# The expert layers of a mixture-of-experts block, computed on the transposed side, with the gate weights fetched by copy and the token weights found from the tokens' side

## The chip, the cores and the metric

One core of one Trainium2 chip runs the whole kernel. The number that counts is the device time of one execution in microseconds (us). The span in a profile is the time from the first to the last instruction of a core.

The engines are called PE (matrix products and transposes; PEld is its loading of weights), ACT (activations and copies), DVE (elementwise work and reductions), POOL (here nearly only indirect DMAs, and some elementwise steps) and SP (it issues the direct DMAs). Each has a queue of its own and takes its instructions in order.

## The reference, cut to what matters

The input is 16 batches of 512 tokens of 128 numbers. Each batch passes an attention layer with 16 heads and then a mixture of 160 experts, of which each token uses 8.

```python
h = layernorm(x) * (1 + ca) + sa;   x = x + ga * attention(h)
h = layernorm(x) * (1 + cb) + sb;   x = x + gb * ffn(h)

def ffn(x):                                     # x: tokens x 128
    probs = sigmoid(x @ router_w.T + expert_bias)      # tokens x 160
    top_w, top_idx = top_k(probs, 8)
    top_w = 2.5 * top_w / (sum(top_w) + 1e-9)
    # for each of a token's 8 experts e with weight w:
    #   routed += w * (silu(x @ w_gate[e].T) @ w_down[e].T)     64 inner numbers
    shared = silu(x @ w_gate_shared.T) @ w_down_shared.T
    return routed + shared
```

## The kernel before

**Two stages.** From 0 to about 974 us the kernel computes attention for the 16 batches, 64 groups of four heads in all. In the gaps of that work it also routes finished batches. From 974 us on it runs the loop over the *quads*, which is the expert layer, and ends with a tail in which only gathers are left.

**Routing.** `route` (lines 520 to 593) computes the router's logits of a batch, turns them into `key = -(1 + exp(-logit))`, finds the 8 largest per token, makes a mask `m` of them and, from their reciprocals, one factor per token (`scale`). The batches form groups of 4, 4, 4, 3 and 1. When all batches of a group are routed, `place` (595 to 718) sorts the group's (token, expert) pairs into *slots*. Two neighbouring experts make a *pair*; a block of 128 slots belongs to one pair, so that one product of 128 columns serves both experts of it. `place` writes, per slot, which of the two halves has to be masked (`away`, from `lim`), and which pair each block has (`pid`).

**Scatter and gather.** Each routed batch is copied to its slots in DRAM by 32 indirect DMAs (`scattering`, line 741: 4 blocks of 128 tokens by 8 experts). After a group's quads, 32 indirect DMAs per batch fetch the results back (`gathering`, line 950), eight to a tile `got`. `combine` (962) adds these eight, multiplies by the token's factor and the gate, and adds the sum to the residual `xr`. There are 512 scatters and 512 gathers. All are issued by POOL.

**A quad** is four blocks of 128 slots. There are 190 in the main loop (44, 44, 44, 36 and 22 in the five groups) and a few spare ones behind a branch. One quad goes through these stages, each in another turn of the loop:

- `load` fetches 512 slots (`xs`), `load_down` the down weights of four pairs (`wd`); both are direct DMAs of 256 KB on SP's queue.
- `turn`: four PE transposes; ACT copies them to `xT`.
- `up`: for each of the four blocks a product with `xT` as the stationary operand and the pair's gate weights, straight out of the resident table `wg` at an address from a register, as the moving one (130 columns: two more hold the router's columns of the pair). After each comes a bf16 product with `away` that adds a huge negative number to the half that does not belong to the slot. DVE adds `shift` to the two router columns (`z`), and ACT applies Silu to the rest (`su`).
- `begin_weights` and `end_weights`: six small DVE steps and one of ACT per two quads find each slot's own weight `w` from `z`.
- `back`: four PE transposes of `su`; DVE copies them to `hwT`.
- `down`: four products with `hwT`; DVE multiplies the result by `w` into `y`, and SP stores it.

**The order** of the work is written out by the loop at line 1160, one turn per quad, with the stages of different quads side by side. Before the `down` of a quad PE reads eight numbers into registers (`name_up`, `name_down`). Side work (routing, placing, the shared expert) is kept in a list of generators, of which `steps.tick` runs up to two steps a turn.

**The planner** (`Steps`, line 1217) keeps a planned time: products advance it (`steps.work`), and it may never lie more than `AHEAD` = 3 us behind the planned ends of DVE and ACT. The `Pacer` (994) emits indirect DMAs by that planned time:

```python
def __call__(self):
    while steps.now >= self.due:
        self.due = max(self.due, steps.now - 4 * self.pace) + self.pace
        if stream(*self.sources) is None:
            break
```

In the quad loop the pace is `PACE_SLOTS` = 0.9 planned us per indirect DMA, scatters first and gathers when no scatter is ready. Each of these DMAs waits for the last PE instruction that was emitted before it (`paced`, 227). `add_up(LAG)` (1151) emits a `combine` as soon as more than `LAG` = 4 complete sets of eight gathers are emitted, so that DVE meets it some sets later; at the end of the loop it takes the rest.

```python
for i in range(-3, len(quads) + 7):
    for stage, q in (("load", i + 3), ("load_down", i - 3), ("name_up", i - 1),
                     ("name_down", i - 5), ("end_weights", i - 4), ("begin_weights", i - 3),
                     ("turn", i), ("up", i - 2), ("back", i - 4), ("down", i - 6)):
        ...
    prepare_sums(); steps.tick(); pacer(); add_up(LAG)
```

Helpers that record nearly all work share their lines: products stand on line 104, transposes on 111, DVE's and ACT's steps on 1212.

Of the kernel before, what the change touches and what calls it, by code (L numbers as in the profile page):

```python
# [19 lines left out]
NB = 16  # L20
S = 512
# [17 lines left out]
TINY = 1e-30  # L39
LAG = 4  # L40

PACE, PACE_SLOTS = 1.3, 0.9
# [28 lines left out]
def block_kernel(ctx: ExitStack, tc: tile.TileContext, t: dict, out: bass.AP):  # L71
# [88 lines left out]
    def load_rest():  # L160
        c.wrout = load("wroutT", [D, E])
        c.wgs = load("wgsT", [D, I])
        c.wds = load("wdsT", [I, D])
        c.bias_p = load("bias_p", [NC, 2])
        c.ones = load("ones", [P, 1])
        c.earlier = load("earlier", [P, P], BF)
        c.many = load("many", [1, P], BF)
        c.pairs = load("pairs", [NC, 2, NC])
        c.spread = load("spread", [NC, 2, E])
        c.table = load("table", [P, 2, NKM])  # L170
# [316 lines left out]
    rows = [tc.dram_tile([P, NBLK, D], FP, name=f"rows{b}") for b in range(NB)]  # L487

    somes = const.tile([1, len(GROUPS)], I32, tag="somes", name="somes")

    class Group:
        def __init__(self, g):
# [4 lines left out]
            self.scale = sb.tile([P, self.tb], FP, tag=f"scale{g}", name="scale")  # L497
            self.idx = sb.tile([P, self.tb, TOPK], I32, tag=f"idx{g}", name="idx")
            self.shift = sb.tile([P, self.nk, 2], FP, tag=f"shift{g}", name="shift")
            self.pid = sb.tile([1, self.nq, 9], I32, tag=f"pid{g}", name="pid")  # L500
            self.some = somes[:, g : g + 1]
            self.away = sb.tile(
                [P, -(-2 * self.nk // P), P], BF, tag=f"away{g}", name="away"
            )
            self.m, self.before = [], []
            self.xg = tc.dram_tile([self.nk * P, D], FP, name=f"xg{g}")
# [13 lines left out]
    def route(gr, i):  # L520
# [40 lines left out]
        yield  # L561

        top = sb.tile([P, NBLK, TOPK], FP, tag="top", name="top")
        for j in range(NBLK):
            vec.max(top[:, j, :], key[:, j, :])
            vec.match_replace(
                out=key[:, j, :], in_to_replace=top[:, j, :], in_values=key[:, j, :], imm_value=1.0
            )
            if j % 2:
                yield  # L570
        m = sb.tile([P, NBLK, E], BF, tag="m", name="m", bufs=max(GROUPS) + 2)
        vec.tensor_scalar(m, key, 0.0, None, ALU.is_gt)
# [13 lines left out]
        yield  # L586

        rs = gr.scale[:, i * NBLK : (i + 1) * NBLK]
        vec.reciprocal(top, top)
        vec.tensor_reduce(rs, top, AX.X, ALU.add, negate=True)  # L590
        vec.tensor_scalar(rs, rs, TOPK_EPS, None, ALU.add)
        vec.reciprocal(rs, rs)
        vec.tensor_scalar(rs, rs, ROUTED, None, ALU.mult)

    def place(gr):
# [41 lines left out]

# [58 lines left out]
        lim = gr.shift[:, :nk, :]  # L696
# [6 lines left out]
        vec.tensor_scalar(lim, lim, 1.0, FAR, ALU.subtract, ALU.mult)  # L703

        flat = tmp([P, 2 * NKM], BF, "flat")[:, : 2 * nk]
        vec.tensor_copy(flat, lim.rearrange("p n a -> p (n a)"))
        yield "o"
        pa = bank([P, -(-2 * NKM // P) * P], BF)
        for n, c0 in enumerate(range(0, 2 * nk, P)):
            k = min(P, 2 * nk - c0)  # L710
            turned(pa[:k, n * P : (n + 1) * P], flat[:, c0 : c0 + k], c.identb)
            vec.tensor_copy(gr.away[:k, n, :], pa[:k, n * P : (n + 1) * P])
        yield "o"
        for a in range(2):
            pl = bank([P, nk])
            mm(pl, c.bias_p[:, a : a + 1].broadcast_to([NC, P]), of)
            vec.tensor_tensor(lim[:, :, a], pl, lim[:, :, a], ALU.add)
            yield "o"
# [40 lines left out]
    class Quad:  # L759
# [17 lines left out]
        ALONE = {"xs": "a", "xT": "b", "su": "a", "wd": "c", "hwT": "b", "y": "a"}  # L777
# [11 lines left out]

        def load_down(self):  # L790
            (p0,) = self.numbers(SP, 0, 1, NC - 4)
            self.wd = self.tile([P, 4, D], "wd", 5)
            nc.sync.dma_start(out=self.wd, in_=t["wdT"][:, bass.ds(p0, 4), :])

        def turn(self):
            pt = now.ps.tile([P, S], FP, tag="turn", name="turn")
# [5 lines left out]
        def name_up(self):  # L802
            self.pids = self.numbers(PE, 1, 4, NC - 1)

        def up(self):

            pu = bank2().rearrange("p a (j n) -> p (a j) n", j=2)
            for j in range(4):
                mm(
                    pu[:, j, 0 : P + 2],  # L810
                    self.xT[:, j * P : (j + 1) * P],
                    wg[:, bass.ds(self.pids[j], 1), :].rearrange("p o n -> p (o n)"),
                    j % 2 == 0,
                    False,
                )
                n, k = divmod(4 * self.q + j, P // 2)
                rows_ = min(P, 2 * self.gr.nk - n * P)
                mm(
                    pu[:, j, 0:P].rearrange("p (a i) -> p a i", a=2),
                    self.gr.away[:rows_, n, :],  # L820
                    c.identb[:rows_, 2 * k : 2 * k + 2].unsqueeze(2).broadcast_to([rows_, 2, I]),
                    False,
                    j % 2 == 1,
                )

            if self.alone or self.q % 2 == 0:
                self.z = self.tile([P, 2, 4, 2], "z", 3)
            else:
                self.z = self.other.z
            vec.tensor_tensor(  # L830
                self.z[:, self.q % 2],
                pu[:, :, P : P + 2],
                self.gr.shift[:, 4 * self.q : 4 * self.q + 4, :],
                ALU.add,
            )
            self.u = self.tile([P, 4, P], "su", 3)
            act.activation(self.u, pu[:, :, 0:P], AF.Silu)

        def begin_weights(self):

            if self.q % 2 == 0 and not self.alone:
                return
            of = slice(self.q % 2, self.q % 2 + 1) if self.alone else slice(0, 2)
            z = self.tile([P, 2, 4], "z1", 3)
            self.w = self.tile([P, 2, 4], "w", 4)
            if not self.alone:
                self.other.w = self.w
            self.s = self.tile([P, 2, 4], "sz", 3)
            z, w = z[:, of], self.w[:, of]
            vec.tensor_tensor(z, self.z[:, of, :, 0], self.z[:, of, :, 1], ALU.max)  # L850
            vec.tensor_scalar(w, z, 0.0, TINY, ALU.is_equal, ALU.mult)
            vec.tensor_tensor(z, z, w, ALU.add)
            vec.reciprocal(w, z)
            act.activation(self.s[:, of], z, AF.Silu)

        def end_weights(self):
            if self.q % 2 or self.alone:
                of = slice(self.q % 2, self.q % 2 + 1) if self.alone else slice(0, 2)
                vec.tensor_tensor(self.w[:, of], self.w[:, of], self.s[:, of], ALU.mult)

        def back(self):
            pt = now.ps.tile([P, S], FP, tag="back", name="back")
            for j in range(4):
                turned(pt[:, j * P : (j + 1) * P], self.u[:, j, :], c.ident)
            self.hT = self.tile([P, S], "hwT", 3)
            vec.tensor_copy(self.hT, pt)
# [4 lines left out]
        def down(self):  # L871
            py = now.ps.tile([P, S], FP, tag="down", name="down")
            for j in range(4):
                mm(
                    py[:, j * D : (j + 1) * D],
                    self.hT[:, j * P : (j + 1) * P],
# [3 lines left out]
            vec.tensor_tensor(  # L880
                y,
                py.rearrange("p (n d) -> p n d", d=D),
                self.w[:, self.q % 2].unsqueeze(2).broadcast_to([P, 4, D]),
                ALU.mult,
            )
# [4 lines left out]
    def spare_quads(gr):  # L890
# [5 lines left out]
        with tc.If(some != 0):  # L896
            for q in range(gr.nq - spare(gr.size), gr.nq):
                quad = Quad(gr, q)
                quad.alone = True
                for stage in ("load", "load_down", "turn", "name_up", "up", "name_down"):  # L900
                    getattr(quad, stage)()
                quad.begin_weights()
                quad.end_weights()
# [508 lines left out]
```

## Time and profile before

| | us |
|---|---|
| median of 3 runs | 1918.97 (1918.86 to 1922.9) |
| the profiled execution | 1925.86 |
| its span | 1924.1 |
| PE busy | 1584.2 |
| DVE busy | 1253.8 |
| ACT busy | 826.6 |
| POOL busy | 1117.9 |

The profiled execution is 6.9 us above the median, and its span is 1.8 us below its own time. Mean granted clock of PE over the span: 0.934. POOL's busy time holds only the executing part of an indirect DMA; a further 0.30 us passes between two of them even when nothing is waited for.

### The profile page before, as it was taken

What the parts mean: (1) busy time and instruction counts of PE and PEld (TensorE: products, weight loads), DVE (VectorE), ACT (ScalarE), POOL (GpSimd) and SP (SyncE); (2) the same over time, 40 slices, a digit from 0 to 9 for tenths busy, and PEclk for the clock granted to TensorE, in tenths of its full rate; (3) what the DMA queues carried; (4) which work ended last, traced back from release to release, by engine and by line L of the source; (5) the groups of instructions that cost most, each with busy time, mean ns of one, the idle gap of its engine ahead of it and who ended that gap; (6) DMA issues with size and microseconds to landing.
All of it is one profiled execution on the core that took longest, in us unless ns stands there. A gap on an engine that the chain in (4) does not pass through costs nothing. (4 is left out here: it accounts for less than half of the span.)

```text
span 1924.1 us, 38397 instructions
## 1 busy us (share of the span) xinstructions
PE 1584.2 (82%) x12683; PEld 1133.7 (59%) x12747; DVE 1253.8 (65%) x3325; ACT 826.6 (43%) x1366; POOL 1117.9 (58%) x1139
## 2 busy tenths in 40 slices
PE   2799999998999989999888887888898878878700
PEld 1355555554555545555468776777788777777600
DVE  2677888887788867787636554546576656666622
ACT  1366666655666556664544332333233323323100
POOL 4001111047775477845657476777777777777776
PEclk8799999998999999999999898999899989999855
DMA  2456555565676667843257676778688878878622
GB/s 83 105 175 201 170 174 170 163 197 177 191 234 188 199 192 219 262 127 117 77 185 244 197 251 203 240 246 275 214 266 272 258 225 272 255 251 254 196 58 57
DMA packets 246678, 377.03 MB, mean 196 GB/s; under 512 B 37604, under 2 KB 136261, under 8 KB 246469
## 3 DMA queue, kind: packets, MB, share of 16 engines
q1 hardware_dynamic: 213700, 307.17, 51.4%
q0 software_dynamic: 32768, 67.17, 12.1%
q8 instruction: 119, 1.95, 0.4%
q14 instruction: 91, 0.74, 0.1%
HBM read 195.15 MB, written 178.26 MB: 194 GB/s over the span
## 5 line engine op out<-in xcount | busy, mean ns | idle before, releaser
L741 POOL DMA_INDIRECT xg<-hs,idx x512 | 493.4, 964 | 284.5 <-issue 95.0
L950 POOL DMA_INDIRECT got<-yg,idx x512 | 491.5, 960 | 156.7 <-issue 123.5
L1212 DVE TENSOR_REDUCE mins<-s 128x2 f32<-128x1024 f32 (+3 forms) x448 | 395.9, 913 | 123.5 <-PE s L104 121.7
L1212 ACT ACTIVATE pT<-s 128x1024 f32<-128x1024 f32 x320 | 323.0, 1021 | 176.7 <-PE s L104 172.3
L104 PE MATMUL s<-wg,xT 128*128 x1520 | 279.6, 307 | 0.6 <-issue 0.6
L104 PEld LDWEIGHTS s<-wg,xT 128*128 128x128 f32 x1520 | 241.6, 200 | 11.3 <-issue 1.2
L111 PE MATMUL turn<-ident,xs 128*128 128x128 f32 x760 | 123.8, 287 | 121.8 <-issue 49.7
L104 PE MATMUL s<-krep,qrep 96*128 96x512 bf16 (+3 forms) x1024 | 197.8, 306 | 31.9 <-DMA qrep<-parts 19.0
L104 PE MATMUL down<-wd,hwT 128*128 x1520 | 206.6, 280 | 3.7 <-DVE y L1212 3.7
L235 POOL TENSOR_TENSOR rot<-rot,three 128x512 f32<-128x512 f32 x32 | 36.8, 1160 | 291.4 <-ACT three L1212 289.4
L104 PE MATMUL s<-qrep,krep 128*128 128x128 bf16 (+3 forms) x960 | 181.6, 299 | 25.3 <-DVE mins L1212 12.3
L104 PE MATMUL av<-pT,v 128*32 128x512 f32 (+3 forms) x2048 | 193.4, 449 | 0.0
L104 PEld LDWEIGHTS down<-wd,hwT 128*128 128x128 f32 x1520 | 190.8, 197 | 4.1 <-DVE y L1212 4.0
L1212 ACT COPY xT<-turn 128x512 f32<-128x512 f32 x190 | 109.8, 578 | 164.8 <-PE turn L111 161.8
L111 PEld LDWEIGHTS turn<-ident,xs 128*128 128x128 f32 x760 | 85.6, 145 | 156.8 <-issue 116.4
L1212 DVE TENSOR_TENSOR z<-s,shift 128x8 f32<-128x8 f32 x190 | 29.6, 156 | 219.3 <-PE s L104 206.5
L104 PEld LDWEIGHTS <-identb 128*128 128x128 bf16 x1280 | 122.0, 100 | 84.9 <-issue 7.0
L104 PE MATMUL s<-identb,away 128*128 128x128 bf16 (+1 forms) x760 | 171.2, 225 | 0.0
L1212 ACT ACTIVATE su<-s 128x512 f32<-128x512 f32 x190 | 113.6, 598 | 129.3 <-DVE z L1212 121.8
L1212 DVE COPY hwT<-back 128x512 f32<-128x512 f32 x190 | 131.0, 689 | 44.2 <-PE back L111 43.6
L1212 DVE TENSOR_TENSOR y<-down,w 128x512 f32<-128x512 f32 x190 | 131.2, 691 | 38.5 <-PE down L104 33.6
L104 PEld LDWEIGHTS <-qrep 96*128 96x128 bf16 x1024 | 83.6, 99 | 119.7 <-issue 95.5
(179 smaller groups left out, 2356.6 us busy)
## 6 DMA issues: line engine op xcount, KB each, us to landing
xg<-zeros SPq DMA_DIRECT2D x228, 256.0 KB
xs<-xg SPq DMA_DIRECT2D x190, 256.0 KB
wd<-in_wdT SPq DMA_DIRECT2D x190, 256.0 KB
yg<-y SPq DMA_DIRECT2D x190, 256.0 KB
krep<-parts SPq DMA_DIRECT2D x64, 288.0 KB
qrep<-parts SPq DMA_DIRECT2D x192, 96.0 KB
parts<-three SPq DMA_DIRECT2D x96, 128.0 KB
yg<-zeros SPq DMA_DIRECT2D x38, 256.0 KB
```

What stands on the lines that cost most here:

```text
L104: steps.last = nc.tensor.matmul(out_, lhsT=lhsT, rhs=rhs, start=start, stop=stop).ins
L111: steps.last = nc.tensor.transpose(out_, in_, ident).ins
L235: in_order(getattr(nc.gpsimd, op)(*args).ins)
L741: s = nc.gpsimd.indirect_dma_start(out=gr.xg, out_offset=bass.IndirectOffsetOnAxis(ap=gr.idx[:, NBLK * i + j, k : k + 1], axis=0), in_=h[: ...
L950: s = nc.gpsimd.indirect_dma_start(out=got[:, k, :], out_offset=None, in_=gr.yg, in_offset=bass.IndirectOffsetOnAxis(ap=gr.idx[:, NBLK * i ...
L1212: return getattr(self.engine, op)(*args, **kwargs)
```

## The change

The first layer is computed transposed. `fetch_up` copies the four pairs' gate weights of a quad into a tile `wq`, two with ACT and two with DVE, each at an address from a register of that engine; PE no longer reads these numbers. In `up` the copied weights are the stationary operand and `xT` the moving one, so that the result has the 128 inner numbers as partitions and can be the stationary operand of `down` as it is: `back` and `hwT` are gone. The mask comes from one bf16 product of two rows (`half`, 2 x 128, with `hide`, 2 x 512) per quad. `hide` is written to DRAM by `place` and fetched for two quads at a time by `load_hide`. `down` no longer weighs; ACT copies its result.

The weights move to the tokens' side: `route` stores `key` and the mask in DRAM, and a new generator `weights` per batch takes them back, finds the eight weights of a token in the order of its eight gathers and normalizes them. `combine` multiplies the eight gathered rows by them before it adds. The pace goes from 0.9 to 0.75, `LAG` from 4 to 3, and some buffer counts change.

```diff
-LAG = 4
-PACE, PACE_SLOTS = 1.3, 0.9
+LAG = 3
+PACE, PACE_SLOTS = 1.3, 0.75
# route
+        nc.sync.dma_start(out=keys[b], in_=key)
...
+        nc.sync.dma_start(out=chosen[b], in_=m)
-        rs = gr.scale[:, i * NBLK : (i + 1) * NBLK]
-        vec.reciprocal(top, top)
-        vec.tensor_reduce(rs, top, AX.X, ALU.add, negate=True)
...
# place
-            vec.tensor_copy(gr.away[:k, n, :], pa[:k, n * P : (n + 1) * P])
-            mm(pl, c.bias_p[:, a : a + 1].broadcast_to([NC, P]), of)
-            vec.tensor_tensor(lim[:, :, a], pl, lim[:, :, a], ALU.add)
+            hide = sb.tile([P, P], BF, tag="hide", name="hide", bufs=2)
+            vec.tensor_copy(hide[:k], pa[:k, n * P : (n + 1) * P])
+            for a in range(2):
+                nc.sync.dma_start(out=gr.hide[a, ...], in_=hide[a:k:2])
# Quad
+        def load_hide(self):
+            if self.q % 2 == 0:
+                two = moe.sb.tile([2, 2, S], BF, tag="hides", name="hides", bufs=3)
+                nc.sync.dma_start(out=two, in_=self.gr.hide[:, at]...)
-        def name_up(self):
-            self.pids = self.numbers(PE, 1, 4, NC - 1)
+        def fetch_up(self):
+            self.wq = self.tile([P, 4, P], "wq", 3)
+            for engine, copy, at in (
+                (mybir.EngineType.Activation, act.copy, 0),
+                (mybir.EngineType.DVE, vec.tensor_copy, 2),
+            ):
+                for j, pid in enumerate(self.numbers(engine, 1 + at, 2, NC - 1), at):
+                    copy(self.wq[:, j, :], wg[:, bass.ds(pid, 1), :]...)
         def up(self):
-                mm(pu[:, j, 0 : P + 2], self.xT[:, j * P : (j + 1) * P], wg[:, bass.ds(self.pids[j], 1), :]..., j % 2 == 0, False)
-                mm(pu[:, j, 0:P]..., self.gr.away[:rows_, n, :], c.identb[:rows_, 2 * k : 2 * k + 2]..., False, j % 2 == 1)
-            vec.tensor_tensor(self.z[:, self.q % 2], pu[:, :, P : P + 2], self.gr.shift[...], ALU.add)
-            act.activation(self.u, pu[:, :, 0:P], AF.Silu)
+            pu = now.ps.tile([P, S], FP, tag="up", name="up", bufs=2)
+            for j in range(4):
+                mm(pu[:, j * P : (j + 1) * P], self.wq[:, j, :],
+                   self.xT[:, j * P : (j + 1) * P], j == 0, False)
+            mm(pu, c.half, self.hide, False, True)
+            self.u = self.tile([P, S], "su", 3)
+            act.activation(self.u, pu, AF.Silu)
-        def begin_weights(self):
...
-        def end_weights(self):
...
-        def back(self):
-                turned(pt[:, j * P : (j + 1) * P], self.u[:, j, :], c.ident)
-            vec.tensor_copy(self.hT, pt)
         def down(self):
-                    self.hT[:, j * P : (j + 1) * P],
+                    self.u[:, j * P : (j + 1) * P],
-            vec.tensor_tensor(y, py..., self.w[...].broadcast_to([P, 4, D]), ALU.mult)
+            act.copy(y.rearrange("p n d -> p (n d)"), py)
+    def weights(b):
...
+        nc.sync.dma_start(out=key, in_=keys[b])
+        nc.sync.dma_start(out=m, in_=chosen[b])
+        yield LATER
+        vec.tensor_tensor(base, m, c.high.unsqueeze(1).broadcast_to([P, NBLK, E]), ALU.mult)
+        for n, (by, mask) in enumerate(((16, 0x7FFF), (0, 0xFFFF))):
+            vec.tensor_scalar(digit, bits, by, mask, ALU.logical_shift_right, ALU.bitwise_and)
+            vec.tensor_tensor(both, base, digit, ALU.add)
+            for j in range(NBLK):
+                vec.max(eight[:, n, j, :], both[:, j, :])
...
+        vec.reciprocal(w, two[:, 0].bitcast(FP))
...
     def combine(gr, i, j, got):
+        vec.tensor_tensor(got, got, w[:, j, :].unsqueeze(2).broadcast_to([P, TOPK, D]), ALU.mult)
         for n in (4, 2, 1):
             vec.tensor_tensor(got[:, 0:n, :], got[:, 0:n, :], got[:, n : 2 * n, :], ALU.add)
-        vec.scalar_tensor_tensor(got[:, 2, :], got[:, 0, :], gr.scale[...], gate, ALU.mult, ALU.mult)
+        vec.tensor_tensor(got[:, 0, :], got[:, 0, :], gate, ALU.mult)
# loop
-    for i in range(-3, len(quads) + 7):
+    for i in range(-3, len(quads) + 5):
+            ("load", i + 3), ("load_hide", i), ("load_down", i - 1), ("fetch_up", i),
+            ("turn", i), ("up", i - 2), ("name_down", i - 3), ("down", i - 4),
```

The small steps of `weights` that are left out number ten and work on 4 to 64 numbers per partition. Buffers: `wd` 5 to 4, `xr` 4 to 3, `got` (`LAG` + 2) 6 to 5; in PSUM `turn` 1 to 2, `up` new with 2, `s` 2 to 1.

## The prediction

> **What bounds the kernel now.** I read the page's busy slices first. The span has two parts: up to about 974 us PE is full, and after that POOL shows a steady 7, hardly broken to the end.
>
> ```profile
> PE   2799999998999989999888887888898878878700
> POOL 4001111047775477845657476777777777777776
> ```
>
> A steady 7 can be a full engine: 0.94 us of work and 0.30 us between two transfers make 0.76. The chain of work that ended last and the windows view settle it.
>
> ```profile
> POOL 3%; issue 1%; DMA 1%; PE 0%; DVE 0%; POOLq 0%; ACT 0%; DVEq 0%
> 1094.50:1300.00 205.50, 168.85 (x1394) 154.90 (x1393) 104.78 (x331) 57.46 (x117) 146.41 (x154) 0.94 0.73 233
> 1300.00:1800.00 500.00, 423.19 (x3446) 387.71 (x3445) 320.48 (x913) 158.19 (x328) 379.32 (x395) 0.96 0.81 253
> 1800.00:1924.00 124.00, 15.43 (x88) 11.82 (x87) 36.87 (x89) 2.67 (x6) 88.41 (x93) 0.55 0.30 82
> ```
>
> The columns are stretch, length, then PE, PEld, DVE, ACT, POOL (busy us and instructions), granted clock, DMA share, GB/s. POOL issues 395 gathers in 500 us, one per 1.265, and goes on at that rate after the quads have ended at 1818. The waits of POOL from 1285 to 1917 say it outright: of its idle time, 393 gaps are the bare 0.3.
>
> ```profile
> POOL got L950 <- issue: 119.8, 393, 0.3
> ```
>
> So the end is set by POOL's queue, and PE's share of 85% in the quad loop sets it only where POOL has to wait for the quads. Such pauses lie before 1285. The longest is here, in POOL's own timeline, where the scatters of the fourth group are not yet placed:
>
> ```profile
> 1075.04 0.96 POOL L741 DMA_INDIRECT xg<-hs,idx  x1 [0.30 <-issue]
> 1094.55 0.96 POOL L741 DMA_INDIRECT xg<-hs,idx  x1 [18.55 <-DVE w L1212]
> ```
>
> POOL's account after the attention: it starts at 984.0. From there to 1269.8, where the unbroken gathers begin, it runs 197 scatters and one gather at 1.26 (249.5 us) and two additions of the routing (5.3), so 31 us of the 285.8 are pauses. Then 511 gathers take 646.6 us, to 1916.4. Landing, the last combine and the last store take 7.7 more, to 1924.1.
>
> **The quads.** From 974 to 1818 there are 190, so 4.44 us each. The shortest on PE are 3.08 us: turn 0.44, up with masks 4 x 0.334, back 0.45, down 0.89, read from the starts in PE's timeline. The rest is register reading ahead of `turn` (0.3 to 1 us), the shared expert, and stretches at clock 0.5. The change takes out `back` (0.45) and the four masks (4 x (0.334 - 0.223) = 0.44, with `down` at 0.89 / 4 = 0.223 as the product without a mask), adds one bf16 product of 512 columns (0.25 with its weights; attention products of up to 512 columns last 0.306 each by themselves), and takes four of eight register reads from PE (about 0.3). That makes about 3.5. Against it stand ACT's and DVE's new register reads and copies, an operation with no row before: I bound a quad by 3.2 and 4.4 (no gain) and take 3.5, because ACT's total (`xT` 0.58, `su` 0.60, `y` about 0.58, two copies at the 0.27 of `gate`, reads about 0.4) is 2.7 and DVE loses more (`hwT` 0.69, `y` 0.69, `z` 0.16) than it gets (two copies). A gain of 0.9 us by 190 quads would be 170 us, but the quads are not what ends last. What the end can gain is POOL's 31 us of pauses, no more.
>
> **The pauses after the change.** The early one: the planner sets scatters by planned time. A turn plans 2.36 us of PE and 2.59 of ACT, and at pace 0.75 that is 3.5 transfers, where before 2.8 / 0.9 gave 3.1. The 69 scatters that are ready at 974 last POOL until about 1076 either way. The fourth group is placed some 25 to 27 turns into the loop; at 3.5 to 3.9 us a turn that is 1062 to 1079. So 1 us is left of this pause, and the small ones up to 1269, where POOL waited for PE, go too. A new one appears. In turns with gathers DVE's planned time counts, at 0.15 us and n / 960 for a step of n numbers: `combine` 3.17 per set, `weights` 8.8 per batch or 2.2 per set, the copies 0.57 per turn. With r gathers a turn that is 0.67 + r / 8 x 5.4, 3.5 us or 4.7 gathers at r = 4.2; since a turn without a `combine` gives only 3.5 and the pacer never more than 5, the turns worked through one by one give 4.2. That is 4.2 x 1.26 = 5.3 us of POOL per 3.5 us of quad: DVE's queue stands at a `combine` until its set has landed, with the copies of the next quads behind it, PE waits for the copies, and the quads run at POOL's pace. The 256 gathers of the first two groups are then emitted by about turn 123, while the third group is done at turn 135. Twelve turns are 42 us and the store 4 more, against 24 gathers POOL still has queued (`LAG` 3: 30 us) and some 5 us that PE runs ahead: a pause of about 11. Bounds: none at 3.5 gathers a turn; 43 us for all pauses with quads at 4.4. Pauses 31 to 12: 19 us gained, between 31 gained and 12 lost.
>
> **What lengthens POOL's own transfers.** The same timeline shows gathers of 0.94 us, and some longer. These two lines show why:
>
> ```profile
> 1338.64 1.47 DVE L1212 TENSOR_TENSOR got<-got 128x512 f32<-128x512 f32 x3
> 1338.69 1.46 POOL L950 DMA_INDIRECT got<-yg,idx  x1 [0.30 <-DMA got<-yg,idx]
> ```
>
> The first of the three additions (0.70 us) ends at 1339.34; the gather that began inside it takes 0.52 longer, to about the end of that addition less 0.13. Gathers that begin just ahead of an addition keep 0.94. All additions of a `combine` have both inputs in SBUF. From 1300 to 1800 the mean is 0.963 against 0.944 in the tail, 7.5 us for 50 sets, 0.15 each. `combine` now begins with a multiplication of 1024 elements: 0.70 for 512 and 0.43 for 256 make 1.24, as long as POOL's cycle of 1.25. A gather's start falls into it nearly always, and waits (1.24 - 0.13)^2 / 2 / 1.25 = 0.49 us in the mean. The whole old sequence comes to 0.18 in the same way (measured 0.15), the new one to 0.50, so about 0.42: 0.27 by 64 sets is 17 us. In `weights`, three 640-element steps with two inputs per batch (0.82, the row of `key`) cost 0.2 each, two with one input (0.51; five of ten gathers over `m` were long) 0.06 each: with the same reduction 0.5 to 0.6 by 16, 8 us. Together 25; bounds 0 (in the tail a combine starts 0.14 us behind a gather's start, and nothing is lengthened) and 46. The 380 copies of 128 elements on DVE I put at nothing: 90 gathers met `w`, a step of 0.19 us from SBUF to SBUF, and were lengthened by 0.002; by the 0.05 of the 0.51 step, on the 60 gathers that would begin inside one (380 x 0.2 / 1.25), it is 3 us at most.
>
> [...]
>
> **The rest.** In the attention the change drops some small DVE steps and four small products per group beside a PE that is 95% busy: nothing. The last `combine` has the multiplication more: +1.2 us in the tail, on the path. Each batch gives SP two stores and two loads more (0.4 us each), each group up to eight stores of `hide`, and two quads one load of it. What is queued behind them on SP: q and k fetches four groups ahead in the attention; `xs` three turns and `wd` three turns ahead in the loop. SP's three issues per quad take about 1.1 of 4.4 us. So I cost them at nothing; without that cover they cost up to 0.4 us each, some 13 us for the 32 stores in the attention. DMA share is 0.81, and the new traffic (16 x 0.5 MB each way) adds 2%.
>
> [...] Here the clock is 0.55 in the tail and 0.96 in the loop. [...]
>
> **Sum.** -19 (pauses) + 25 (longer transfers) + 1 (tail) = +7 us. The profiled execution goes from 1925.86 to 1933, the median from 1918.97 to 1926.
>
> **The rivals.**
> - *Faster: the lengthening is small.* If gathers land so that the multiplication ends just as the next one starts, as in the tail, the term falls from 25 to about 5. The pauses gained then decide: -19 + 5 + 1 = -13, or -25 if no new pause appears (all 31 gained): 1906 down to 1894. For it: the offset in the tail is fixed. Against it: under load the gathers' packets end 2.2 to 4.6 us after the start of the gather, so the phase is spread. It wins where the lengthening stays below 14 us.
> - *Slower: the quads gain nothing.* If register reads and copies on ACT and DVE, or one PSUM buffer for `down`, keep a quad at 4.4 us, the pauses are 43 instead of 31: +12 + 25 + 1 = +38, 1957. For it: PE's register reads cost 0.3 to 1 us a quad now. Against: ACT's 2.7 us.
> - *No change:* gain and lengthening cancel within 4 us. PE's work falls, and POOL's 1024 transfers end where they ended.
>
> **How the numbers follow.** A measurement of this kernel tells 0.2% (3.8 us) from no change. My forecast, slower by a few us, has 0.40, quads without gain 0.16, faster 0.29, no change 0.15. That makes 0.29, 0.15 and 0.56. The likeliest case has its own range of 1923 to 1945; over all cases 8 in 10 lie from 1897 to 1953, which takes in nearly all of the faster rival and the slower one up to 4 us below its own 1957.
>
> **What would show it.** Right: no `back`, quads on PE near 3.5 us where DVE does not stand; POOL without the pause at 1075 and with one near the third group's end; gathers with a mean near 1.0 and single ones up to 2 us; DVE's multiplications waiting for gathers in mid-loop. Wrong: gathers still at 0.96 (faster), POOL waiting often for PE (slower than I say), or an attention part that is longer.

## The result, and the profile after

The change makes the kernel slower: median 1948.57 us (1947.37 to 1952.06, 4 runs) against 1918.91 (1916.91 to 1922.9, 4 runs) for the kernel before, ratio 1.0155 with an interval of 1.0134 to 1.0176. That is 29.7 us where 7 were forecast. The profiled execution took 1948.75 us, its span 1946.6, mean granted clock 0.898 (before 0.934). Of the 29.7 us the two profiled spans show 22.5 (1946.6 - 1924.1); the rest is that the profiled execution before lay 6.9 us above its median and this one 0.2.

The busy slices of the page after, PE and POOL:

```profile
PE   2799999998999989999795978994756677477800
POOL 4001111157773677737477177777777777777776
```

POOL is again a steady 7 to the end, but there is a 1 in its 23rd slice, from 1071 to 1119 us. PE has a 5 in the slice before that (1022 to 1071), and is no longer full behind the 27th. The chain of waits and the windows (stretch, length, PE, PEld, DVE, ACT, POOL busy with instructions, clock, DMA share, GB/s) of the kernel after:

```profile
PE 3%; POOL 2%; issue 1%; DMA 1%; DVE 1%; SPq 0%; POOLq 0%; ACT 0%; ACTq 0%; DVEq 0%
```

```profile
1110.00:1300.00 190.00, 166.00 (x1215) 139.41 (x1214) 62.90 (x239) 114.02 (x270) 144.84 (x149) 0.96 0.87 285
1300.00:1800.00 500.00, 330.78 (x2118) 276.34 (x2117) 262.79 (x709) 215.58 (x499) 383.31 (x383) 0.81 0.72 226
1800.00:1947.00 147.00, 45.20 (x290) 37.26 (x290) 75.32 (x183) 27.38 (x61) 105.36 (x108) 0.64 0.44 135
```

From 1300 to 1800 PE is down to 331 us from 423, yet POOL gets 383 instructions through where it got 395: a transfer every 1.305 us instead of 1.265. POOL's waits from 1285 on are still the bare issue gap:

```profile
POOL got L961 <- issue: 119.2, 391, 0.3
```

The pause that was to vanish is in POOL's timeline, more than twice as long as the 18.5 us before, and a line of PE's timeline stands beside it:

```profile
1062.90 0.95 POOL L739 DMA_INDIRECT xg<-hs,idx  x1 [0.30 <-issue]
1063.87 2.62 POOL L235 TENSOR_TENSOR h<-h,row 128x512 f32<-128x512 f32 x2
1066.64 1.01 POOL L739 DMA_INDIRECT xg<-hs,idx  x1 [0.15 <-issue]
1108.65 0.95 POOL L739 DMA_INDIRECT xg<-hs,idx  x1 [41.00 <-PE turn L110]
```

```profile
1066.54 1.11 PE L110 MATMUL s<-ident,h 128*128 128x128 f32 x4 [19.52 <-POOL h L235]
```

PE stood for 19.5 us on `h`, the normalized rows of a batch in late routing, because the multiplication and the addition that make `h` (2.62 us together) lay behind scatters in POOL's queue. What the prediction calls "two additions of the routing (5.3)" is two such pairs, one for each of two batches. In the kernel before the same product of PE stands at 1059.13 with no such wait.

POOL's account, by its lines after the attention:

| us | before | after | difference |
|---|---|---|---|
| first scatter of the expert stage | 984.0 | 975.5 | -8.5 |
| pauses above the 0.30 of issue | 31 | 42.9 (2.2 and 40.7) | +12 |
| 512 gathers, mean of one | 0.960 | 0.996 | +18.7 in all |
| scatters (197, 195), mean of one | 0.959 | 0.971 | +2 for length, -2.5 for number |
| last gather to end of span | 7.7 | 8.6 | +0.9 |

The sum is +22.6, against 22.5 measured. The first row need not come from the change. Two of the kernels below run the same attention as the kernel before, and there this scatter starts at 977.0 and at 983.1. So a difference of some 7 us lies between executions, and the profiled execution before was 6.9 us above its median.

### The profile page after: what moved, and what is told of

It reads as the page before. It is cut to its first block, busy times and chain, and to the rows that moved or that the text cites. A ratio compares the mean times of both kernels' runs of the same rounds, so it can differ in the third digit from the quotient of the medians.

```text
span 1946.6 us, 36098 instructions
## 1 busy us (share of the span) xinstructions
PE 1522.8 (78%) x11397; PEld 1028.2 (53%) x11397; DVE 1146.2 (59%) x2997; ACT 998.5 (51%) x1841; POOL 1141.1 (59%) x1139
## 5 line engine op out<-in xcount | busy, mean ns | idle before, releaser
L961 POOL DMA_INDIRECT got<-yg,idx x512 | 510.2, 996 | 156.0 <-issue 130.1
L103 PE MATMUL up<-xT,wq 128*128 128x128 f32 x1520 | 225.1, 294 | 45.3 <-DVE wq L1217 45.3
L103 PE MATMUL down<-wd,su 128*128 x1520 | 231.0, 297 | 27.1 <-ACT su L1217 6.7
L103 PEld LDWEIGHTS down<-wd,su 128*128 128x128 f32 x1520 | 194.3, 200 | 91.5 <-issue 34.9
L103 PEld LDWEIGHTS up<-xT,wq 128*128 128x128 f32 x1520 | 206.6, 210 | 48.9 <-DVE wq L1217 48.0
L103 PE MATMUL s<-qrep,krep 128*128 128x512 bf16 (+3 forms) x1024 | 195.1, 303 | 20.5 <-DVE mins L1217 7.7
L1217 DVE COPY wq<-wg 128x128 f32 x380 | 75.4, 250 | 187.9 <-PE up L103 113.9
L1217 ACT COPY y<-down 128x512 f32<-128x512 f32 x190 | 111.5, 587 | 142.0 <-PE down L103 98.3
L1217 DVE TENSOR_TENSOR got<-got,w 128x1024 f32<-128x1024 f32 x64 | 78.4, 1225 | 159.9 <-DMA got<-yg,idx 158.4
L1217 ACT ACTIVATE su<-up 128x512 f32<-128x512 f32 x190 | 113.7, 599 | 103.7 <-PE up L103 102.9
L103 PEld LDWEIGHTS <-krep 128*128 128x128 bf16 x1024 | 84.9, 98 | 65.8 <-issue 39.0
L110 PEld LDWEIGHTS turn<-ident,xs 128*128 128x128 f32 x760 | 97.3, 154 | 36.6 <-issue 24.7
```

The source lines that it names most:

```text
L103: steps.last = nc.tensor.matmul(out_, lhsT=lhsT, rhs=rhs, start=start, stop=stop).ins
L110: steps.last = nc.tensor.transpose(out_, in_, ident).ins
L961: s = nc.gpsimd.indirect_dma_start(out=got[:, k, :], out_offset=None, in_=gr.yg, in_offset=bass.IndirectOffsetOnAxis(ap=gr.idx[:, NBLK * i ...
L1217: return getattr(self.engine, op)(*args, **kwargs)
```

## The experiments

The theory after the result: the end is still set by POOL's queue, and the loss has two separate terms there, a pause in which the fourth group's scatters are late (by the order of issue, and by PE standing on `h`), and gathers lengthened by `combine`'s long two-input multiplication. The rival: the new form of the quads itself (copies of the weights, register reads on ACT and DVE) is what is late.

The runs fell on four chips, with the kernel before run on each beside them. On the first it took 1920.29 us and on the third 1921.64; on the second 2195.95 and on the fourth 2217.69. The runs on the second and the fourth are told of apart, at the end.

### The multiplication alone, in the kernel before

```diff
     def combine(gr, i, j, got):
+        nc.vector.tensor_tensor(got, got, eights[:, :].unsqueeze(2).broadcast_to([P, TOPK, D]), ALU.mult)
```

> The kernel before, with one step more in each combine: DVE multiplies the 8 gathered rows by a tile of ones (128 x 1024, both inputs in SBUF), nothing else. Theory (a two-input DVE step holds up a gather that starts inside it): the mean gather between 1300 and 1800 us rises from 0.963 to about 0.99, some gathers last up to 2 us, and the time rises by 0.27 x 52 + 1 = 15 us (8 to 25). Rival (DVE's step does not touch POOL, it only costs DVE time, which has room): only the last combine shows, +1.2 us, and the mean gather stays at 0.96.

Measured: 1935.77 us, ratio 1.0078 (1.0054 to 1.0101), 15.5 us slower. The groups of instructions, here the gathers of the kernel before and of this one (busy us, mean ns, then idle time ahead of them):

```profile
L950 POOL DMA_INDIRECT got<-yg,idx x512 | 491.5, 960 | 156.7 <-issue 123.5
```

```profile
L952 POOL DMA_INDIRECT got<-yg,idx x512 | 507.8, 992 | 160.8 <-issue 120.4
```

The 512 gathers took 16.3 us more (507.8 - 491.5), which is the whole difference; the pauses, counted as in the table above, were 31.2 us against 31.1 before. One more DVE instruction of 1.22 us per `combine`, 64 in all, on an engine with idle time costs this much, by lengthening POOL's transfers. The rival (+1.2 us and gathers at 0.96) is out.

### The multiplication taken out of the changed kernel

```diff
-        vec.tensor_tensor(got, got, w[...].broadcast_to([P, TOPK, D]), ALU.mult)
-        for n in (4, 2, 1):
-            vec.tensor_tensor(got[:, 0:n, :], got[:, 0:n, :], got[:, n : 2 * n, :], ALU.add)
+        vec.tensor_scalar(got[:, 0, :], got[:, 0, :], w[:, j, 0:1], None, ALU.mult)
+        for n in range(1, TOPK):
+            vec.scalar_tensor_tensor(got[:, 0, :], got[:, n, :], w[:, j, n : n + 1],
+                                     got[:, 0, :], ALU.mult, ALU.add)
```

> The changed kernel, with the 1024-element multiplication and the three additions of combine replaced by one multiplication and seven multiply-adds of 128 elements each (about 0.3 us each, total DVE time about the same). Theory (a gather waits for the rest of a two-input step that is running when it starts): short steps leave a short rest, the mean gather falls from 1.00 to about 0.97 and the time by 10 to 18 us. Rival (what lengthens gathers is DMA load or DVE's total time): mean gather and time stay within 4 us.

Measured: 1930.22 us, ratio 1.0046 (1.0027 to 1.0066). Against 1.0155 for the change that is 0.0109 of 1919, 21 us (18 by the medians alone). The gathers of the changed kernel and of this one:

```profile
L961 POOL DMA_INDIRECT got<-yg,idx x512 | 510.2, 996 | 156.0 <-issue 130.1
```

```profile
L961 POOL DMA_INDIRECT got<-yg,idx x512 | 495.3, 967 | 156.1 <-issue 118.0 <-DMA got<-yg,idx 14.6 <-PE up L103 9.4
```

Same arithmetic, DVE no less busy (1153 us against 1146), and 15 us less on POOL, so it is the length of the single step that counts and not DVE's total. The pause stayed at 41.4. The two terms are separate.

### The pause: more side steps a turn, and the rows moved off POOL

```diff
-        steps.tick()
+        steps.tick(3)
```

> The changed kernel, with up to three instead of two steps of side work in each turn of the quad loop. In the order of issue the fourth group's first scatter moves from turn 33 to turn 28 (28 in the kernel before). Theory (the 41 us pause of POOL comes from the weights generator of batch 0 taking side-work steps ahead of routing and placing): the pause shrinks by 5 turns of 3.5 us, 17 us, and the time by 10 to 20 us, some of it given back if a pause at the end of the third group appears. Rival (the pause is PE standing 19.5 us for the routed rows that POOL has queued behind scatters): the stand stays, the pause shrinks by less than 8 us.

Measured: 1938.03 us, ratio 1.009 (1.0062 to 1.0117), 12 us below the change (0.0065 of 1919).

```diff
-        side("tensor_tensor", h, h, row[:, 1:2, :].broadcast_to(full), ALU.mult)
-        yield side("tensor_tensor", h, h, row[:, 0:1, :].broadcast_to(full), ALU.add) + 1.5
+        if moe.sb is None:
...
+        else:
+            vec.tensor_tensor(h, h, row[:, 1:2, :].broadcast_to(full), ALU.mult)
+            vec.tensor_tensor(h, h, row[:, 0:1, :].broadcast_to(full), ALU.add)
+            yield
```

`moe.sb` is None until the quad loop begins; up to there the two lines taken out (shown as `...`) still run.

> The changed kernel, with the two row steps of the last batch's routing (multiply and add of 128 x 512, 1.3 us each on POOL) done by DVE once the quad loop has begun. In the order of issue the fourth group's first scatter moves from turn 33 to 29. Theory (PE stands 19.5 us at the transposes of these rows because POOL works through its queued scatters first, and the turn of placing is late): no stand of PE at these transposes, the pause of 41 us falls to about 8, the time by 20 to 35 us less what a new pause at the end of the third group takes (about 10). Rival (the pause only moves, because the quads that follow are what the gathers wait for): the time changes by less than 8 us.

Measured: 1924.58 us, ratio 1.0014 (0.9993 to 1.0035), 27 us below the change, most of its loss. The end of the pause in POOL's timeline, with three steps and with the rows on DVE:

```profile
1093.09 1.00 POOL L739 DMA_INDIRECT xg<-hs,idx  x1 [28.30 <-PE up L103]
```

```profile
1090.68 0.96 POOL L744 DMA_INDIRECT xg<-hs,idx  x1 [19.67 <-DVE wq L1222]
```

41 us became 28 and 19. With three steps PE still stood 16.8 us on `h`, as the rival there had it, yet the pause shrank by 13 us (17 expected). With the rows on DVE PE did not stand there, and moving four row steps of 5.3 us in all off POOL gave five times that; the pause of about 8 that was expected was missed. The planner's order moved with it: the fourth group's first scatter came at turn 29 instead of 33, at turn 28 with three steps. The profiled execution of the second was 16 us above its median with gathers at 1.016, so only its pause is read here, and its time from the median.

### All edits at once

The short steps, the three side steps a turn and the rows on DVE come together with a fourth edit. It limits what the planner adds to the due time of a side step (`steps.most` is 9.0 until the quad loop):

```diff
+    steps.most = 0.5
     for i in range(-3, len(quads) + 5):
...
-            after = self.now + self.behind()
+            after = self.now + min(self.behind(), self.most)
```

> The kernel with short multiply-adds, three side steps a turn, row steps on DVE and the planned delay limited to 0.5 us once more, because on the chip of the runs just before the kernel before took 2196 us instead of 1920 and POOL's queue stopped for 1.5 to 2 us every 10 us there. If the kernel before takes about 1920 us here: theory (pause and lengthening are the two terms that the change lost) no pause over 5 us, gathers 0.97, span about 1887, ratio 0.980 to 0.988. Rival (without the pause POOL runs ahead of the quads and waits for them later): a pause of 10 us or more behind 1285, ratio 0.99 or above. If it takes about 2196 us: ratio 0.998 to 1.006 as before, and nothing is told apart.

Measured, with the kernel before at 1921.64: 1901.00 us, ratio 0.9892 (0.9874 to 0.9911). This beats both kernels, by 20.6 us the one before and, by the ratios, by 2.6% the changed one. The quads have their new form in it, so that form is not what made the change slower. The ratio lies between the theory's range of 0.980 to 0.988 and the rival's 0.99, and the windows of busy time and POOL's timeline show that the pause which the rival named did come:

```profile
1300.00:1800.00 500.00, 394.12 (x2511) 329.82 (x2512) 290.90 (x988) 252.67 (x584) 367.51 (x377) 0.86 0.79 253
```

```profile
1548.10 0.95 POOL L966 DMA_INDIRECT got<-yg,idx  x1 [0.30 <-issue]
1567.17 0.94 POOL L966 DMA_INDIRECT got<-yg,idx  x1 [18.12 <-DVE got L1223]
```

The early pause is gone (0.7 us at 1150 is left), and a pause of 17.8 us stands at the third group's end, where POOL has worked off the gathers of two groups. DVE's timeline has a pair of `wq` copies every 2.73 us from 1548 to 1559, so the quads ran at their own speed there, and were late: the third group's last `y` starts at 1560.3. One thing that had held them shows in PE's waits from 974 to 1285:

```profile
PE up L103 <- DMA hides<-hide: 28.0, 4, 16.1
```

PE stood 28 us on the masks that `load_hide` fetches, for 16.1 and 10.6 us at 1105 and 1146. SP's queue stood just before, for 12.7 and 10.5 us, at the load of the next batch's rows (`hs`), which waited for scatters to be done with that tile; the fetch of the masks lay behind it. In the changed kernel SP's queue stands 14.9 us, in 6 times, at that load until scatters are done, and PE 10.1 us on the masks in the same stretch. How much of the 17.8 us comes from this was not varied.

Account against the changed kernel, to the last gather: start +0.5, pauses -24.4, gathers -12.6 (497.6 against 510.2), scatters -2, row steps off POOL -5.3: -43.8, and the last gather ends 43.9 us earlier (1938.0 to 1894.1).

### The masks left out of the kernel before

```diff
-                mm(pu[:, j, 0:P]..., self.gr.away[:rows_, n, :], c.identb[...], False, j % 2 == 1)
+                steps.work(128 / 2400)
```

> The kernel before with the four mask products of every quad left out once more (the masks are not applied; 84 us of PE less, same order of issue). If the kernel before takes about 1920 us here: theory (POOL's queue sets the end) POOL unbroken from 1270 on and gathers at 0.96, at most 10 of the 31 us of pauses gone, ratio 0.994 to 1.001, quads ending at most 10 us earlier than 1818. Rival (PE bounds the quad loop): ratio below 0.98. If it takes about 2196 us: 0.990 as there, since with POOL's stops the quads are what is late.

Measured, on the same chip as the last: 1913.38 us, ratio 0.9948 (0.9932 to 0.9964), 8 us faster. From POOL's waits over the whole span (123.5 us, 405 times in the kernel before) and the windows of this kernel:

```profile
POOL got L944 <- issue: 123.2, 404, 0.3
```

```profile
1300.00:1800.00 500.00, 389.45 (x3010) 358.21 (x3010) 324.19 (x929) 156.15 (x326) 380.05 (x394) 0.94 0.80 255
```

The pauses fell from 31 to 22 us, and that is the gain. 84 us of PE taken away moved the last `y` of the quads 23 us forward (1816 to 1793; the expectation said 10 at most), the gathers stayed at 0.960 us, and the end moved 8. So PE is not what bounds the kernel before.

### On the two slower chips

Six runs fell there. They are listed with the kernel before of the same chip as 1.

| | chip | median us | ratio |
|---|---|---|---|
| planned delay limited, in the changed kernel | second | 2197.66 | 1.0007 (0.9984 to 1.0031) |
| short steps, three side steps, rows on DVE | second | 2209.29 | 1.0060 (1.0035 to 1.0084) |
| all four edits | second | 2201.75 | 1.0021 (1.0000 to 1.0041) |
| kernel before without masks | second | 2175.66 | 0.9904 (0.9878 to 0.9930) |
| all four edits, pace 0.9 | fourth | 2183.25 | 0.9832 (0.9778 to 0.9886) |
| kernel before, three edits | fourth | 2220.72 | 1.0011 (0.9991 to 1.0031) |

> The changed kernel, with the planned delay of a side step in the quad loop limited to 0.5 us (the planner otherwise adds how far DVE's and ACT's planned ends lie ahead). All instructions are the same; only the order changes: the first scatter of the fourth group is emitted at turn 24 instead of 33, the last of the third group at turn 19 as before. Theory (the pause of 41 us comes from the turn at which the fourth group is placed and from the stand on h): three steps a turn moved that scatter by 5 turns and the pause by 13 us, 2.6 us a turn, so 9 turns take 23 us: pause about 18, gathers still 0.995, time about +0.4% against the kernel before (+7 us, between 0 and +15). Rival (the placing's own work on the chip lasts that long, whatever the order): pause over 33 us, time +1.2% or more.

> The changed kernel with three earlier edits at once: combine by a multiply and seven multiply-adds of 128 elements, three side steps a turn, and the two row steps of the late routing on DVE. First scatter of the fourth group at turn 26. Theory (two independent terms, the pause and the lengthening of gathers): gathers at 0.97 (-18 us against the changed kernel), pause 10 to 15 us (-28), sum -46 +- 8, which is 16 us below the kernel before, ratio 0.988 to 0.996. Rival (the pause taken away early comes back as a wait for the quads before the gathers of a group, since POOL's queue would then run ahead of the quads): a new pause of 10 us or more behind 1300, ratio 1.000 or above.

> As the run before it (short multiply-adds, three side steps a turn, row steps on DVE) with the planned delay of side steps limited to 0.5 us too: first scatter of the fourth group at turn 19, one turn behind the last of the third group. Theory: no pause over 5 us, POOL's 1024 transfers back to back from 975 on: 975.5 + 192 scatters and 3 others at 1.265 (247) + 512 gathers at 1.27 (650) + additions of the routing 5 + tail 9 = a span of about 1887, ratio 0.980 to 0.988. Rival (quads then too slow to feed POOL): pauses come back at the end of a group, time no better than with three edits.

> The kernel before with the four mask products of every quad left out (their planned time kept, so that the order of issue is the same): the masks are not applied in it. That takes 4 x 0.11 us of PE from each of 190 quads, 84 us in all. Theory (POOL's queue of transfers sets the end, PE only the pauses ahead of 1285): some of the small pauses on PE go, at most 10 of the 31 us; quads end up to 10 us earlier or not at all; ratio 0.994 to 1.001. Rival (PE's 85% in the quad loop bounds): 40 us or more faster, ratio below 0.98.

The first keeps to its pause and time (an early pause of 18.8 us, at 1188, and 1.7 us slower), but its gathers have a mean of 1.011, not 0.995, and it has late pauses of 34 and 21 us that it did not expect; the theories of the other three miss. The second meets its rival (late pauses of 24 and 22 us), the fourth lies between theory and rival. The chip is the reason that can be seen: a quad takes 5.5 us there (all four edits: from the first `xT` at 1058 to the eighty-first at 1499), and POOL waits for the quads. In POOL's timeline of the run with all four edits the third group's end looks like this:

```profile
1802.30 0.94 POOL L966 DMA_INDIRECT got<-yg,idx  x1 [44.44 <-PE up L103]
```

Where the quads are late, time won earlier on POOL comes back as a wait at the next group's end, so these runs say nothing of the loss on the other chips. They do show the rival of the combined run at work: without the masks, which makes quads shorter, 20 us are won here and 8 there.

> As the run with all four edits of the changed kernel, with the pace of indirect DMAs back at 0.9 instead of 0.75, because that run gave a pause of 17.8 us at 1567, where POOL had finished the gathers of two groups and the third group's quads were not done. At pace 0.9 the gathers of the first two groups are emitted by turn 136 instead of 122, so fewer of DVE's combines stand ahead of the third group's weight copies. First scatter of the fourth group at turn 21. Theory (the late pause comes from gathers issued ahead of the quads): late pause 0 to 10 us, nothing else changed, ratio 0.980 to 0.987. Rival (the quads' own speed sets when the third group is done): late pause 15 us or more, ratio 0.988 or above.

```diff
-PACE, PACE_SLOTS = 1.3, 0.75
+PACE, PACE_SLOTS = 1.3, 0.9
```

Measured: 0.9832, and behind 1200 no pause longer than 3 us, where the same kernel at pace 0.75 had pauses of 44, 17 and 10 on the second chip. The quads ran faster too, 4.7 us each between the forty-first and the eighty-first `xT` against 5.4. That speaks for the theory (gathers issued ahead of the quads make the late pause), but it compares two chips, and what it gives where the kernel before takes 1920 us was not measured.

> The kernel before with the edits against the early pause: three side steps a turn, row steps on DVE, planned delay limited to 0.5 us. First scatter of the fourth group at turn 21 instead of 28, one turn behind the last of the third. Theory (POOL's queue ends last in the kernel before as well): the early pause of 18 us falls below 6, gathers stay at 0.96; the third group's quads then come about 12 us late, a new pause of 5 to 15 us behind 1500; ratio 0.985 to 0.997, so most of the best time belongs to the edits and not to the change. Rival (the faster quads of the change are what makes the edits pay): pauses of 25 us or more in all behind 1285, ratio 0.998 or above.

Measured: 1.0011, which is in the rival's range; but the expectation was made from the timing of the other chips, so this decides little. Its own late pause is 24.7 us at 1819. On this chip, at one pace, the changed kernel with four edits takes 2183 us and the kernel before with three 2221 (the short steps have no counterpart there). Whether the kernel before would gain from the three edits at 1920 us stays open, and so does how much of the best time belongs to the change.

## Why the prediction was right and wrong

**POOL's queue sets the end: right.** The masks' run shows it from before, the gathers' account from after: what changes in POOL's transfers or pauses comes out in the time to a few us, and 84 us taken from PE moved it by 8, which is what POOL's pauses lost.

**The early pause of 1 us: wrong, and this is the step that failed.** The prediction kept 1 of the 31 us of early pauses; 42.9 were measured. With the late pause of 11 the term stood at -19 in the sum, and it came out as +12. The prediction had the fourth group placed "some 25 to 27 turns into the loop; at 3.5 to 3.9 us a turn". By the order in which the kernels issue, its first scatter came at turn 33 (in the kernel before at turn 28), and the turns up to there took 4.0 us (1108.7 less 975.5, over 33), with the 19.5 us in which PE stood on `h` in them. The timelines agree: 30 `xT` copies had started by that scatter in the kernel before, and 35 after. So the row at 1094.55 that the prediction shows already had more turns ahead of it than 25 to 27. It booked the row steps on POOL as 5.3 us of POOL's time and did not ask who waits for them behind POOL's queue; at pace 0.75 that queue is given 3.5 x 1.26 = 4.4 us of work a turn where a turn was to take 3.5. And it gave the new generator `weights` a price for DVE's steps, but none for the places it takes among two side steps a turn, ahead of `place`. The runs with three steps and with the rows on DVE show that turn and stand each carry a part: five turns less with the stand left took 13 us off the pause, four turns less without the stand 21. That the pace of 0.75 made the stand is read from the timelines only; it was not varied alone.

**The late pause of 11: not in the changed kernel, but real.** POOL came to the third group's gathers at 1606, and that group's last `y` had started at 1586, so the quads were done by then. With the early pause taken away it appeared at 1567 with 17.8 us. The late pause had been forecast for a kernel without the early one, so the prediction's own argument (what is late next) was not tested by the change alone; its 11 us against 17.8 are of the right kind, from a kernel with four more edits.

**The lengthened gathers: right in mechanism and size.** 25 was forecast and 20.7 measured (18.7 on gathers, 2 on scatters). The multiplication was put at 17: 16.3 on the gathers when added to the kernel before, 15 when cut into short steps. `weights` was put at 8: the 45 transfers that met its 640-element addition were 0.13 us longer each and the 46 that met its shifts 0.06, some 9 us, and the 23 that met its third two-input step (`base`) about 0.08, 2 us more; all of this is an upper bound, since other steps overlap with them. The rule for a start inside a step (the gather ends 0.94 us after the end of that step less 0.13, or after its own start where that is later) held for 62 of the 64 transfers that began inside a multiplication of the changed kernel, to 0.04 us; two that began within 0.04 us of its start kept 0.94. One of the 62, in lines of DVE's and POOL's timelines:

```profile
1515.88 1.22 DVE L1217 TENSOR_TENSOR got<-got,w 128x1024 f32<-128x1024 f32 x1 [0.16 <-issue]
```

```profile
1516.49 1.43 POOL L961 DMA_INDIRECT got<-yg,idx  x1 [0.30 <-issue]
```

The multiplication ends at 1517.10; less 0.13 that is 1516.97, and 0.94 from there is 1517.91. The gather ended at 1517.92. The faster rival needed a fixed offset between the two and a term of about 5; it fell with the 20.7.

**The copies of the weights at nothing: right.** The 176 transfers that met a `wq` copy were 0.025 us longer in the mean, some 4 us in all at most.

**Quads of 3.5 us: near.** Between the forty-first and the eighty-first `xT` a quad took 3.75 us (1128 to 1278) against 4.45 before (1144 to 1322). Where nothing held it, as from 1030 to 1036, PE began a quad's `up` every 2.73 us, against the 3.08 that the prediction read before. The masks' one product, put at 0.25 there, took 0.32 to the start of the next product (1031.45 to 1031.77); no run shows 0.25. Later the quads ran at POOL's pace, with DVE standing 105 us in 29 waits for gathers between 1300 and 1800, as forecast. The slower rival had pauses of 43 us by quads without a gain: the number was met, the reason was not.

**The granted clock** fell from 0.96 to 0.81 between 1300 and 1800, with POOL unbroken there (from 1285 on none of its gaps is longer than 0.3 us), so POOL's account has no term for it.

**The rest.** The expert stage began 8.5 us earlier on POOL, and the attention was put at no change; the first `xT` came at 970 instead of 975. By the starts at 977 and 983 in other runs of the same attention, most of this can be a difference of executions. The tail had +1.2 forecast and +0.9 measured. SP's added transfers were put at nothing. They left no pause on POOL that the account needs, but PE stood 10.1 us on the masks between 974 and 1285, and 28 with all four edits.

Put together: +7 forecast, +31 for the early and late pauses (-19 against +12), -8.5 for the start, -4 for the lengthening, -2.5 for two scatters fewer after it: 23, and the spans differ by 22.5. The measured 1948.6 us lie outside the likeliest case's own range of 1923 to 1945, and inside the wide one of 1897 to 1953 only because that took in most of the slower rival, whose reason (quads without gain) did not occur. That the number lies there is luck.

## What to carry to other kernels

Where an in-order queue sets the end, ask of each instruction in it not only what it takes but who waits for it at the far end: a multiplication and an addition of 2.6 us together, behind a queue of scatters, held another engine for 19.5 us, and moving such steps to an engine with idle time, with the order of issue that followed, was worth about 27. The same came again on SP's queue, where a load that waited for scatters held the masks behind it, and PE stood 28 us. A pause in such a queue hid the next one, here of 17.8 us, so a run that takes a pause away has to be read for where POOL stops next. And beside a stream of indirect transfers, eight short DVE steps instead of a long one and a tree of additions gave 15 us of POOL's time for the same arithmetic.

## What had not been expected of the hardware

The same kernel took 1920 us on two chips and 2196 and 2218 on two others. There POOL's run of transfers is cut about every 10 to 13 us, and ACT, DVE and POOL go on within 0.4 us of each other, as in these lines of the timeline of the run with all four edits on the second chip:

```profile
1373.18 0.94 POOL L966 DMA_INDIRECT got<-yg,idx  x1 [0.31 <-issue]
...
1375.63 0.60 ACT L1223 ACTIVATE su<-up 128x512 f32<-128x512 f32 x1 [3.07 <-remote]
1375.67 0.36 DVE L1223 COPY wq<-wg 128x128 f32 x2 [8.55 <-remote]
...
1375.96 0.94 POOL L966 DMA_INDIRECT got<-yg,idx  x1 [1.84 <-remote]
...
1376.76 1.16 PE L103 MATMUL down<-wd,su 128*128 x8 [3.28 <-ACT y L1223]
```

POOL stands 1.8 us at this cut where 0.3 is usual, and the kernel before without masks has such cuts as well (1.82 us at 1356, 2.05 at 1569); the instructions themselves keep their durations (0.94 for a gather, 1.16 for `down`). What causes the cuts is not settled by any run here.
